# Conditioning by rows in three float32r passes, input checks moved behind, output chunks ended one by one

## The chip, the cores and the metric

The kernel runs on one core of a Trainium2 chip. The metric is the device time of one execution in microseconds (us), as the median of several runs. A profiled execution gives, beside its own time, the start and end of every instruction on the engines: PE (TensorE; PEld is its weight load), DVE (VectorE), ACT (ScalarE), POOL (GpSimd), and SP, which here only issues DMAs.

## The reference

The input x has 8 rows of 128 tokens with 512 features, all float32. Two layers are added to it, each a conditioning followed by a feed-forward network. Cut to the core:

```python
# layer 0
base = einsum('btd,od->bto', x, W)
logits = einsum('btd,ed->bte', x, Wr) + 5.0 * one_hot(language_ids)      # 8 experts
gates = softmax over the two largest logits, zero for the others
lora = einsum('bter,bte,eor->bto', einsum('btd,erd->bter', x, A), gates, B)
c = base + 2.0 * lora
w = scales[g_idx] * (nibbles - (zeros[g_idx] + 1))                       # 4-bit weights
x = x + down(silu(gate(c)) * up(c))                                      # 512 -> 1376 -> 512
# layer 1
c = einsum('bsi,boi->bso', x, weight[adapter_ids])                       # one of 8 matrices by row
c = rms_norm(c) * ln_w
x = x + down(silu(gate(c)) * up(c))                                      # 512 -> 1792 -> 512
```

## The kernel before

All activations are kept transposed: features on the 128 partitions in four chunks (KC = 4), the 1024 tokens along the free axis, in two halves of 512 (NTB = 2, TB = 512). A half has four rows of x.

A product that must be exact to float32 can be had in two ways here. A plain float32 matmul is one instruction that the hardware runs as two records. Or both operands are split into a high part in float32r, a low part and a scaled combination (`a3[0]`, `a3[1]`, and a third), and float32r matmuls over the parts are summed in PSUM, with a rescale of the PSUM bank between the passes. The layer 1 network works with three such passes (L924, L988). The layer 0 network needs two, because its dequantised integers are exact, and rescales the sums from one group of scales to the next by `ratio` and `ratio_d`.

The condition of layer 0, one half after the other: `experts(tb)` (L286) multiplies each row by `wa`, the router and all low-rank A matrices side by side (136 columns). `gated(tb, banks)` computes on DVE the two best experts and their softmax, with one Exp on ACT (L315), and multiplies the low-rank products by the gates (`hg`). `condition(tb, hg)` computes `base` in plain float32 (L349), transposes `hg` on PE (L346), copies it to SBUF and adds the low-rank part with `bT` (L359). `split_condition` writes the high part on ACT (L619) and the low part on DVE (L620); these feed the gate and up products of layer 0 (L485). x arrives by chunk and half (`load_x`, L214), chunks 1 and 3 on ACT's queue, the others on SP's; it lies in `xT`, which is also the residual. `wT` is loaded in two halves on the two queues. Until x is there, 13 idle matmuls of 512 columns keep PE busy (L236).

While `base` runs, DVE unpacks zeros and dequantises the first four chunks of gate and up weights (`queue_zeros`, `queue_weights`). After the second half's `experts`, DVE works out the row numbers for gathers (`indices`), the `ratios`, and a `verdict`: whether the group indices and scales are such that the fast way applies. `judge` sums the verdict over the partitions with a tiny matmul (L660) and writes a flag (L661). Then POOL starts the first gathers of layer 1's adapter matrices (`first_w1`, L268).

The orders of PE, DVE and ACT are written out by hand (`manual_schedule`). In the networks, a small planner decides when queued DVE and ACT work is issued: `spent` moves a clock by 0.2326 us for each matmul, `pump` issues queued tasks whose time has come, and `flush` issues a named task at the latest where it is needed. POOL and the DMA queues follow the scheduler's order.

In layer 0, `down` (L532) runs for each output chunk m over halves (`tb`), and inside over the high and the low part of h. `last_chunk_and_down` interleaves the last gate and up chunk with the first products of the last down block. Layer 1 begins with `adapt` (L870) and `normed` (transposes, L889) for each row, then gate and up in 14 chunks, with `down` (L988) after each of four blocks. In the last block, the third pass runs by halves: all four output chunks for the first 512 tokens, then all four for the second; each of the eight results is added to `xT` (L1000) and stored by a DMA of 256 KB (L1021), even m on ACT's queue and odd m on SP's.

At the very end every engine loads the flag (`values_load`, L1061) and branches (L1062): a second, general network in plain float32 follows in the program and runs only if the flag is set. With these inputs it doesn't run.

Of the kernel before, what the change touches and what calls it, by code (L numbers as in the profile page):

```python
# [27 lines left out]
NWARM = 13  # L28
# [38 lines left out]
GU_PLACE, FLAG_PLACE = 64, 24  # L67

AFTER = 0.3

# [13 lines left out]
def network(tc: tile.TileContext, a, out, by_groups, flag=None):  # L84


    with ExitStack() as ctx:
        network_in(ctx, tc, a, out, by_groups, flag)


def network_in(ctx, tc, a, out, by_groups, flag):
# [111 lines left out]

    xsrc = a["xT"].rearrange("(c p) t -> p c t", p=P)
    wa = cp.tile([P, KC, E + E * R], F32, name="wa")
    wT = cp.tile([P, KC, D], F32, name="wT")
    bT = cp.tile([P, D], F32, name="bT")
    g_idx = const.tile([P, KC + NJ0], I32, name="g_idx")
# [3 lines left out]
    def load_x(c, tb):  # L212
        cols = slice(tb * TB, (tb + 1) * TB)
        (nc.sync, nc.scalar)[c % 2].dma_start(out=xT[:, c, cols], in_=xsrc[:, c, cols])  # L214

    nc.sync.dma_start(out=wa, in_=a["WA"])
    for c in (1, 0, 3, 2):
        load_x(c, 0)
    for half, eng in enumerate((nc.sync, nc.scalar)):
        cs = slice(2 * half, 2 * half + 2)  # L220
        eng.dma_start(out=wT[:, cs, :], in_=a["WT"][:, cs, :])
    nc.sync.dma_start(out=ids[:, 0, :], in_=a["ids0"].partition_broadcast(P))
    for c in (1, 0, 3, 2):
        load_x(c, 1)
    nc.scalar.dma_start(out=bT, in_=a["BT"])
# [4 lines left out]


    ones = cp.tile([P, TB], BF16, name="ones")
    nc.vector.memset(ones, 1.0)
    idle = bank("idle")
    for _ in range(NWARM):
        nc.tensor.matmul(idle, lhsT=ones[:, :P], rhs=ones, start=True, stop=True)  # L236
# [41 lines left out]
    def experts(tb):  # L278

        got = []  # L280
        for i, ps in enumerate(banks_of("experts", TB // T // 2)):
            ps = ps[:, : 2 * (E + E * R)].rearrange("p (b n) -> p b n", b=2)
            for k in range(2):
                b = tb * (TB // T) + 2 * i + k
                for c in range(KC):
                    nc.tensor.matmul(  # L286
                        ps[:, k, :],
                        lhsT=xT[:, c, b * T : (b + 1) * T],
                        rhs=wa[:, c, :],
                        start=(c == 0),  # L290
                        stop=(c == KC - 1),
                    )
            got.append(ps)
        return got
# [42 lines left out]
    def condition(tb, hg, meanwhile=None):  # L337


        small = pair("hgT")  # L340
        hgT = cp.tile([P, TB], F32, tag="hgT", bufs=2, name="hgT_sb")
        base = banks_of("base", KC)
        for m in range(KC):
            if m == KC - 1:
                for i in range(TB // T):
                    nc.tensor.transpose(small[:, 0, i * T : (i + 1) * T], hg[:, i, :], ident)  # L346
                nc.scalar.copy(hgT, small[:, 0, :])
            for c in range(KC):
                nc.tensor.matmul(  # L349
                    base[m],  # L350
                    lhsT=wT[:, c, m * P : (m + 1) * P],
                    rhs=xT[:, c, tb * TB : (tb + 1) * TB],
                    start=(c == 0),
                    stop=False,
                )
        if meanwhile is not None:
            meanwhile(small[:, 1, :])
        for m in range(KC):
            nc.tensor.matmul(  # L359
                base[m], lhsT=bT[:, m * P : (m + 1) * P], rhs=hgT, start=False, stop=True  # L360
            )
        return base
# [31 lines left out]
    def by_groups_of_scales():  # L394
# [26 lines left out]
        )  # L421

# [51 lines left out]
        def ratios():  # L474
            for r, s in ((ratio, sc), (ratio_d, scd)):

                nc.vector.tensor_tensor(r, s[:, :, 1:], s[:, :, 1:], ALU.mult)
                nc.vector.tensor_scalar(r, r, LEAST**2, None, ALU.is_lt)
                nc.vector.tensor_tensor(r, r, s[:, :, 1:], ALU.add)
                nc.vector.reciprocal(r, r)  # L480
                nc.vector.tensor_tensor(r, r, s[:, :, :-1], ALU.mult)
# [47 lines left out]
        def down_product(ps, m, k, tb, first):  # L529
            n = CH0[k]  # L530
            for i in range(2):
                nc.tensor.matmul(  # L532
                    ps[:, tb],
                    lhsT=wds[k][:n, m * P : (m + 1) * P],
                    rhs=h2[k][i][:, tb],
                    start=(first and i == 0),
                    stop=(i == 1),
                    skip_group_check=not first,
                )
            spent(2)  # L540
# [5 lines left out]
        def down(k0, k1):  # L546

            sums = [pair("down") for _ in range(KC)]
            for k in range(k0, k1):
                flush(f"h{k}")  # L550
                for m in range(KC):
                    if m == 1:
                        flush(f"h{min(k + 2, k1 - 1)}")
                    for tb in range(NTB):
                        down_product(sums[m], m, k, tb, k == k0)
                    if k == k1 - 1:
                        down_final(xT[:, m, :].rearrange("p (b t) -> p b t", b=2), m, sums[m], k)
                    else:
                        rescale(sums[m], ratio_d[:, m, k : k + 1])

        def last_chunk_and_down():
# [16 lines left out]
            def first(m):  # L578
                for tb in range(NTB):
                    down_product(sums[m], m, j - 2, tb, True)  # L580
                rescale(sums[m], ratio_d[:, m, j - 2 : j - 1])

            def second(m, tbs=range(NTB)):
                for tb in tbs:
                    down_product(sums[m], m, j - 1, tb, False)
# [24 lines left out]
            for tb in range(NTB):  # L610
                for m in range(KC):
                    down_product(sums[m], m, j, tb, False)
                    down_final(xT[:, m, tb * TB : (tb + 1) * TB], m, sums[m][:, tb], group)

        def split_condition(tb, base):
            cols = slice(tb * TB, (tb + 1) * TB)
            for m in range(KC):
                hi, lo = (x[:, m, cols] for x in a3)
                nc.scalar.activation(hi, base[m], AF.Copy, scale=HSCALE)  # L619
                nc.vector.tensor_tensor(lo, base[m], hi.bitcast(F32), ALU.subtract)  # L620
# [25 lines left out]
        with tc.manual_schedule(engines={EngineType.PE, EngineType.DVE, EngineType.Activation}):  # L646
            hg = gated(0, experts(0))
            queue_zeros(0, 4, "zeros")
            for j in range(4):
                queue_weights(j, f"w{j}")  # L650
            flush("w3")
            split_condition(0, condition(0, hg))
            hg = gated(1, experts(1))
            indices()
            ratios()
            count = verdict()

            def judge(ps):
                met = ps[:1, :1]
                nc.tensor.matmul(met, lhsT=count[:, 0:1], rhs=count[:, 1:2], start=True, stop=True)  # L660
                nc.vector.tensor_scalar(flag[:1], met, float(NGOOD * P), None, ALU.is_lt)  # L661

            split_condition(1, condition(1, hg, judge))
            cond_stack.close()
            first_w1()
# [36 lines left out]
            queue_down(*BLOCKS0[2], "d8")  # L702
            down(*BLOCKS0[1])
            ready(PAIRS0[4])
            gate_up_pair(8, 9)
            ready(PAIRS0[5])
            last_chunk_and_down()


    def in_float32():  # L710
        gp_stack = ExitStack()
        gp = gp_stack.enter_context(tc.tile_pool(name="gp", bufs=1, side="left"))
        ax = gp.tile([P, KC, NT], F32, name="ax")
        for tb in range(NTB):
            hg = gated(tb, experts(tb))
            base = condition(tb, hg)
            for m in range(KC):
                nc.scalar.copy(ax[:, m, tb * TB : (tb + 1) * TB], base[m])
        indices()
        cond_stack.close()  # L720
        h0 = h_stack.enter_context(tc.tile_pool(name="h0", bufs=1, side="right")).tile([P, NJ0, NT], F32, name="h0")
# [66 lines left out]
        nc.sync.dma_start(out=ln_w, in_=a["ln_w"])  # L788
        first_w1()
# [4 lines left out]
    last_silu = [None]  # L794

# [42 lines left out]
    def first_w1():  # L838
        pools["w1"] = w1_stack.enter_context(tc.tile_pool(name="w1", bufs=1, side="right"))
# [46 lines left out]
    def normed(b, nx):  # L886
        pt = bank("nxT")
        for c in range(KC):
            nc.tensor.transpose(pt[:, c * T : (c + 1) * T], nx[:, c * P : (c + 1) * P], ident)  # L889
        raw = ad.tile([P, KC, T], F32, tag="raw", bufs=2, name="raw")  # L890
# [90 lines left out]
    def down(j0, j1):  # L981

        sums = [pair("down") for _ in range(KC)]
        last = j1 == NJ1

        def one(m, tb, j, which):
            for i in which:
                nc.tensor.matmul(  # L988
                    sums[m][:, tb],
# [7 lines left out]

        def done(m, x, ps):
            charge("dve", took("dve", ps.free_size()))
            nc.vector.scalar_tensor_tensor(x, ps, -EPS, x, ALU.mult, ALU.add)  # L1000


        for js in (range(j0, j1 - 1), range(j1 - 1, j1)):
            for m in range(KC):
                for tb in range(NTB):
                    for j in js:
                        one(m, tb, j, (0, 1))
                if j1 - 1 in js:
                    rescale(sums[m], HLSCALE)
        halves = [slice(0, 1), slice(1, 2)] if last else [slice(0, 2)]  # L1010
        for tbs in halves:
            for m in range(KC):
                for tb in range(tbs.start, tbs.stop):
# [179 lines left out]
```

## Time and profile before

| what | us |
|---|---|
| median of 3 runs | 444.04 (443.54 to 444.15) |
| profiled execution, its own time | 444.17 |
| its span, first to last instruction | 442.3 |
| start of the first experts product after the DMA wait | 8.06 |
| start of the first layer 0 gate product on the chain | 50.81 |
| start of layer 1's first gate product on the chain | 205.33 |
| end of the last PE work | 434.77 |
| PE, DVE, ACT, POOL busy | 431.1, 292.9, 213.1, 9.0 |

The profile is of one execution. A line of the table of groups gives the source line, the engine, the operation, what it writes from what it reads, shapes, the count, busy time and the mean time of one, then how long the engine was idle just before these instructions and what ended that idle time. The chain that ended last is followed back from the last instruction, each time to what released it. A float32 matmul appears as two records. A q behind an engine's name means its sequencer or its DMA queue.

### The profile page before, as it was taken

How to read it: one execution, taken by the hardware profiler on the slowest of the kernel's cores; microseconds unless marked ns; L12 is line 12 of the kernel's file. 1: busy time of each engine (PE TensorE's matmuls, PEld its weight loads, DVE VectorE, ACT ScalarE, POOL GpSimd, SP SyncE). 2: the span in 40 equal slices, each digit the busy share in tenths (PEclk: the TensorE clock that was granted, in tenths of full speed). 3: DMA queues.
4: the chain of work that ended last, by engine and by line, in shares of the span. 5: the costliest groups of instructions: out<-in, count | busy, mean ns of one | idle time of the engine just before them, and what ended most of it. 6: DMA issues, size and time to landing. Idle time of an engine off the chain costs nothing.

```text
span 442.3 us, 4678 instructions
## 1 busy us (share of the span) xinstructions
PE 431.1 (97%) x1799; PEld 326.5 (74%) x1799; DVE 292.9 (66%) x418; ACT 213.1 (48%) x242; POOL 9.0 (2%) x20
## 2 busy tenths in 40 slices
PE   7999999999999999999999999999999999999993
PEld 4464578888888866456888888888888888888882
DVE  0767379997999668877449926379626477634643
ACT  1020388867886766446487322475131471325320
POOL 0000200000000000210000000000000000000000
PEclk9999999999999999999999999999999999999998
DMA  8830170101000002870403301113001110000005
GB/s 284 295 96 1 39 294 0 48 20 36 1 0 0 1 0 96 288 282 1 144 0 106 133 0 41 47 50 95 30 1 47 48 50 24 0 1 0 1 0 196
DMA packets 12269, 30.96 MB, mean 70 GB/s; under 512 B 2640, under 2 KB 5200, under 8 KB 11216
## 3 DMA queue, kind: packets, MB, share of 16 engines
q1 hardware_dynamic: 9648, 19.32, 13.5%
q0 software_dynamic: 1152, 8.39, 5.1%
q10 hardware_dynamic: 1440, 2.88, 1.7%
q8 instruction: 16, 0.26, 0.2%
q14 instruction: 13, 0.11, 0.1%
HBM read 28.49 MB, written 2.10 MB: 69 GB/s over the span
## 4 chain that ended last, share of the span: by engine, by line
PE 91%; DVE 4%; DMA 1%; ACT 1%; issue 0%; SPq 0%; DVEq 0%; ACTq 0%
PE gate L924 17%; PE up L924 17%; PE down L988 16%; PE gate L485 9%; PE down L532 8%; PE up L485 8%; PE base L349 6%; PE adapt L870 5%; PE experts L286 2%; PE base L359 2%; DMA xT<-in_xT 1%; DVE xT L1000 1%; DVE xT L544 1%; PE nxT L889 1%; ACT sl L501 1%; DVE h L504 1%
## 5 line engine op out<-in xcount | busy, mean ns | idle before, releaser
L924 PE MATMUL gate<-a,w 128*128 128x512 f32 x336 | 81.7, 390 | 0.0
L924 PE MATMUL up<-a,w 128*128 128x512 f32 x336 | 81.4, 389 | 0.0
L988 PE MATMUL down<-h,d 128*128 128x512 f32 x336 | 76.8, 389 | 0.0
L924 PEld LDWEIGHTS up<-a,w 128*128 128x128 f32 x336 | 63.1, 188 | 13.1
L988 PEld LDWEIGHTS down<-h,d 128*128 128x128 f32 x336 | 63.1, 188 | 13.1
L924 PEld LDWEIGHTS gate<-a,w 128*128 128x128 f32 x336 | 62.7, 188 | 13.5 <-ACT gate L174 0.6
L941 DVE SCALAR_TENSOR_TENSOR h<-up,sl 128x1024 f32<-128x1024 f32 (+1 forms) x16 | 17.5, 1091 | 50.9 <-PE up L924 44.5
L485 PE MATMUL gate<-a,dq 128*128 128x512 f32 (+1 forms) x176 | 48.0, 394 | 0.2
L485 PE MATMUL up<-a,dq 128*128 128x512 f32 (+1 forms) x176 | 47.3, 391 | 0.0
L532 PE MATMUL down<-h,wd 128*128 128x512 f32 (+1 forms) x176 | 42.3, 394 | 0.8 <-DVE h L188 0.7
L532 PEld LDWEIGHTS down<-h,wd 128*128 128x128 f32 (+1 forms) x176 | 32.5, 188 | 9.7 <-DVE h L188 1.1
L485 PEld LDWEIGHTS gate<-a,dq 128*128 128x128 f32 (+1 forms) x176 | 32.4, 185 | 9.0 <-DVE a L620 0.8
L485 PEld LDWEIGHTS up<-a,dq 128*128 128x128 f32 (+1 forms) x176 | 32.5, 185 | 7.7 <-ACT sl L501 0.2
L198 ACT ACTIVATE h<-h 128x1024 fp32r<-128x1024 f32 (+1 forms) x25 | 26.4, 1054 | 15.9 <-DVE h L941 15.5
L188 DVE TENSOR_TENSOR h<-h,h 128x1024 fp32r<-128x1024 f32 (+1 forms) x25 | 30.4, 1217 | 3.4 <-ACT h L198 3.4
L938 ACT ACTIVATE sl<-gate 128x1024 f32<-128x1024 f32 (+1 forms) x16 | 14.7, 918 | 35.7 <-PE gate L924 35.7
L174 ACT ACTIVATE gate<-gate,ratio 128x1024 f32<-128x1024 f32 (+1 forms) x24 | 26.0, 1085 | 11.6 <-PE gate L485 11.6
L870 PE MATMUL adapt<-w,xT 128*128 128x512 f32 x64 | 28.7, 594 | 0.0
L174 ACT ACTIVATE gate<-gate 128x1024 f32<-128x1024 f32 (+1 forms) x15 | 13.8, 923 | 30.8 <-PE gate L924 30.8
L349 PE MATMUL base<-xT,wT 128*128 128x512 f32 x64 | 28.1, 592 | 0.0
L176 DVE TENSOR_SCALAR down<-down 128x1024 f32<-128x1024 f32 x8 | 9.9, 1232 | 26.2 <-PE down L988 26.2
L174 ACT ACTIVATE up<-up,ratio 128x1024 f32<-128x1024 f32 (+1 forms) x21 | 22.7, 1082 | 5.5 <-PE up L485 5.5
(121 smaller groups left out, 442.6 us busy)
## 6 DMA issues: line engine op xcount, KB each, us to landing
wgu<-in_wgu SPq DMA_DIRECT2D x14, 512.0 KB, 3.4
wd<-in_wd SPq DMA_DIRECT2D x6, 512.0 KB, 3.7
qw<-in_qw_gu SPq DMA_DIRECT2D x5, 512.0 KB, 4.2
xT<-in_xT ACTq DMA_DIRECT2D x4, 256.0 KB, 6.0
xT<-in_xT SPq DMA_DIRECT2D x4, 256.0 KB, 5.6
qwd<-in_qw_d SPq DMA_DIRECT2D x2, 512.0 KB, 5.4
out<-xT ACTq DMA_DIRECT2D x4, 256.0 KB, 3.8
out<-xT SPq DMA_DIRECT2D x4, 256.0 KB, 3.9
```

The lines of the kernel that those rows point to most:

```text
L174: nc.scalar.activation(ps, ps, AF.Copy, scale=by)
L176: nc.vector.tensor_scalar(ps, ps, by, None, ALU.mult)
L188: nc.vector.tensor_tensor(lo, x, hi.bitcast(F32), ALU.subtract)
L198: nc.scalar.activation(hi, x, AF.Copy, scale=HSCALE)
L349: nc.tensor.matmul(base[m], lhsT=wT[:, c, m * P : (m + 1) * P], rhs=xT[:, c, tb * TB : (tb + 1) * TB], start=(c == 0), stop=False,)
L485: nc.tensor.matmul(ps, lhsT=dqs[j][:, c, half, :], rhs=a3[i][:, c, tb * TB : (tb + 1) * TB], start=(c == 0 and i == 0), stop=(i == 1), ski ...
L532: nc.tensor.matmul(ps[:, tb], lhsT=wds[k][:n, m * P : (m + 1) * P], rhs=h2[k][i][:, tb], start=(first and i == 0), stop=(i == 1), skip_gro ...
L870: nc.tensor.matmul(ps, lhsT=xT[:, c, b * T : (b + 1) * T], rhs=wt[:, c * D : (c + 1) * D], start=(c == 0), stop=(c == KC - 1),)
L924: nc.tensor.matmul(ps, lhsT=w3[j][i][:, c, half * P : (half + 1) * P], rhs=a3[i][:, c, tb * TB : (tb + 1) * TB], start=(i == 2 and c == 0) ...
L938: nc.scalar.activation(sl, ps, AF.Silu, scale=1.0 + EPS)
L941: nc.vector.scalar_tensor_tensor(h, ps, 1.0 + EPS, sl, ALU.mult, ALU.mult)
L988: nc.tensor.matmul(sums[m][:, tb], lhsT=d3[j][i][:, m * P : (m + 1) * P], rhs=h3[j][i][:, tb], start=(i == 0 and j == j0), stop=(j == j1 - ...
```

## The change

x is loaded a second way: `xb`, the eight rows one by one (256 KB each, alternately on ACT's and SP's queue), laid out by the host. `xT`, now the residual alone, is loaded later by `load_residual` in two DMAs of 1 MB behind `qzd` on SP. `wT` comes by output chunk in four DMAs and `bT` behind them, all on SP. The 26 idle matmuls have 128 columns.

`experts` of both halves come first. `base` is computed in three float32r passes: x and W are split into high, low and combined parts. Shares of the work: `x_high`, `x_scaled`, `w_high`, the scaling of `bT` and the rescale of the sums on ACT; `x_low` of half 0, `w_low` and `w_diff` on DVE; `x_low` of half 1 and `x_diff` of both on POOL. `kept` saves the second half's experts to SBUF so that its PSUM pair is free. The passes of the two halves alternate. `split_condition` treats two output chunks at a time. `ratios` is called in two parts.

`indices` and `first_w1` move to the second down block of layer 0, `verdict` into its last chunk, `judge` into the first `normed` of layer 1. Layer 0's `down` runs over the parts outside and the halves inside. The flag is loaded ahead of layer 1's last down, with a branch hint for PE, DVE and ACT, and the branch at the end falls through into the second network. The last down ends one output chunk after another, only the last one by halves; the first half of a chunk is stored from ACT's queue, the second from SP's. The second network is changed to match.

The instruction streams of the two kernels show what isn't in the diff: POOL runs `x_diff(0)` before `x_low(1)`, then `x_diff(1)`; the first product of base's second pass of half 1 waits for ACT (`x_scaled(1)`), the first of the third pass of half 0 for DVE, ACT and POOL; one rescale of an up sum moves from DVE to ACT beside `indices`; the ten DVE instructions of `verdict` stand right ahead of the last chunk's h.

```diff
-NWARM = 13
+NWARM = 26
...
+FETCHED = [EngineType.PE, EngineType.DVE, EngineType.Activation]
...
-    for c in (1, 0, 3, 2):
-        load_x(c, 0)
...
+    for b in range(B):
+        (nc.scalar, nc.sync)[b % 2].dma_start(
+            out=xb[:, b].rearrange("p c t -> p (c t)"), in_=a["xb"][b]
+        )
+        if b == 3:
+            nc.sync.dma_start(out=ids[:, 0, :], in_=a["ids0"].partition_broadcast(P))
+    for m in range(KC):
+        nc.sync.dma_start(out=wT[:, m, :], in_=a["WT"][:, m, :])
+    nc.sync.dma_start(out=bT, in_=a["BT"])
...
+    def x_high(tb):
+        for b in rows(tb):
+            nc.scalar.activation(x_parts(tb, b)[0], xb[:, b], AF.Copy, scale=HSCALE)
+
+    def x_low(tb, eng):
+        for b in rows(tb):
+            hi, lo, _ = x_parts(tb, b)
+            eng.tensor_tensor(lo, xb[:, b], hi.bitcast(F32), ALU.subtract)
+
+    def x_scaled(tb):
+        for b in rows(tb):
+            lo = x_parts(tb, b)[1]
+            nc.scalar.activation(lo, lo.bitcast(F32), AF.Copy, scale=1.0 / EPS)
+
+    def x_diff(tb):
+        for b in rows(tb):
+            hi, lo, di = x_parts(tb, b)
+            nc.gpsimd.tensor_tensor(di, hi.bitcast(F32), lo.bitcast(F32), ALU.subtract)
...
+    def base_products(base, tb, m, i):
+
+        for c in range(KC):
+            nc.tensor.matmul(
+                base[m],
+                lhsT=wT3[i][:, m, c * P : (c + 1) * P],
+                rhs=x_parts(tb)[i][:, c, :],
...
+            nc.scalar.activation(root, eps, AF.Exp)
+            exp0 = experts(0)
+            x_high(0)
+            x_low(0, nc.vector)
+            x_scaled(0)
+            exp1 = experts(1)
+            for m in range(2):
+                w_high(m)
+            hg0 = gated(0, rows_of(exp0))
+            for m in range(2, KC):
+                w_high(m)
+            kept = cp.tile([P, 2, 2 * (E + E * R)], F32, name="kept")
+            nc.scalar.copy(kept, exp1[:, :, : 2 * (E + E * R)])
+            x_high(1)
+            x_low(1, nc.gpsimd)
+            x_diff(0)
+            scale_bT()
+            pairs0, base0 = base_sums()
+            for m in range(KC):
+                base_products(base0, 0, m, 0)
+            hgT0 = turned(hg0, exp0[:, 0, :])
+            for m in range(KC):
+                w_low(m)
+                base_products(base0, 0, m, 1)
+            hg1 = gated(1, [kept[:, i].rearrange("p (b n) -> p b n", b=2) for i in range(2)])
+            x_scaled(1)
+            x_diff(1)
+            for ps in pairs0:
+                rescale_base(ps)
+            pairs1, base1 = base_sums()
+            for i in range(2):
+                for m in range(KC):
+                    base_products(base1, 1, m, i)
+            for ps in pairs1:
+                rescale_base(ps)
+            for m in range(KC):
+                w_diff(m)
+                base_products(base0, 0, m, 2)
             queue_zeros(0, 4, "zeros")
             for j in range(4):
                 queue_weights(j, f"w{j}")
+            flush("w2")
+            ratios(ratio, sc)
+            for i in range(2):
+                for m in range(2 * i, 2 * i + 2):
+                    low_rank(base0, hgT0, m)
+                split_condition(0, pairs0[i], i)
+            ratios(ratio_d, scd)
             flush("w3")
...
+            base_products(base1, 1, 0, 2)
+            hgT1 = turned(hg1, base0[0])
+            for m in range(1, 3):
+                base_products(base1, 1, m, 2)
+            for i in range(2):
+                for m in range(2 * i, 2 * i + 2):
+                    if m == KC - 2:
+                        base_products(base1, 1, KC - 1, 2)
+                    low_rank(base1, hgT1, m)
+                split_condition(1, pairs1[i], i)
...
             for i in range(2):
+                for tb in tbs:
...
+            queue("dve", "indices", 1.7, indices)
             down(*BLOCKS0[1])
+            flush("indices")
+            first_w1()
...
+            queue("dve", "verdict", 1.3, lambda: count.append(verdict()))
             last_chunk_and_down()
+            flush("verdict")
...
+        if last:
+            for fn in (first, ended):
+                for m in range(KC - 1):
+                    fn(m)
+            for m in range(KC - 2):
+                added(m)
+                for tb in tbs:
+                    store(m, tb)
+            m = KC - 1
+            banks[m, 1] = pair("down")[:, 1]
+            for tb in tbs:
+                passes(m, (tb,), every, (0, 1))
+                rescale(banks[m, tb], HLSCALE)
+            added(m - 1)
+            for tb in tbs:
+                store(m - 1, tb)
+            for tb in tbs:
+                passes(m, (tb,), every, (2,))
+                done(m, xT[:, m, tb * TB : (tb + 1) * TB], banks[m, tb])
+                store(m, tb)
+            return
...
+            if j1 == NJ1 and by_groups:
+                again.append(nc.values_load(flag[:1, :], min_val=0, max_val=1))
+                tc.mark_branch_hint_location("again", hint=again[0], engines=FETCHED)
             down(j0, j1)
...
-    with tc.If(again > 0, preferred_fallthrough_block=False, name="again"):
+    with tc.If(again[0] > 0, preferred_fallthrough_block=True, label="again", name="again"):
```

## The prediction

> **What bounds the kernel now.** I read the page first (shares of busy time), then the chain of waits in order of time, then windows by stage, then the tail's queue instructions. The page:
>
> ```profile
> span 442.3 us, 4678 instructions
> ...
> PE 431.1 (97%) x1799; PEld 326.5 (74%) x1799; DVE 292.9 (66%) x418; ACT 213.1 (48%) x242; POOL 9.0 (2%) x20
> ...
> PE 91%; DVE 4%; DMA 1%; ACT 1%; issue 0%; SPq 0%; DVEq 0%; ACTq 0%
> ```
>
> TensorE is nearly the whole path, so only three things pay: less PE work, an earlier first matmul, a shorter tail. The chain in order of time (start, length, what) shows the head of the kernel:
>
> ```profile
> 1.67 6.36 DMA xT<-in_xT
> 8.06 3.51 PE experts L286 x28
> 11.58 10.30 PE base L349 x24
> 21.88 0.44 PE hgT L346 x4
> 22.31 3.44 PE base L349 x8
> 25.75 3.43 PE base L359 x8
> 29.18 3.71 PE experts L286 x32
> ...
> 47.06 0.12 PE hgT L660 x2
> 47.18 3.63 PE base L359 x8
> 50.81 1.05 PE gate L485 x4
> ...
> 231.68 3.63 PE gate L924 x16
> ```
>
> Read: a DMA holds the first product to 8.06; from there PE never rests until the first gate product at 50.81. A float32 matmul of 512 columns is two records, 3.44/8 = 0.430 each, so 0.86 us; a float32r one is 3.63/16 = 0.2267 us. The windows by stage give 22 us of DVE and 4.5 us of ACT work in the head, POOL none. The tail (PE ends at 434.77) is shown by the stores' landing times and by the final branch:
>
> ```profile
> DMA to landing us min/median/max: 2.1/3.9/4.7
> ...
> L1062 SPq EVENT_SEMAPHORE  x8: 17/17/17, 436.9 to 440.4; - x8
> ...
> L1062 PEldq COMPARE_BRANCH  x2: 95/2282/4468, 434.2 to 435.0; - x2
> ```
>
> The last store is issued at 435.5 and SP waits for landings until 440.2; PE's branch over the second network takes 4.47 us, to 439.5, and DVE drains at 440.1. Two limits end together; 2 us of barrier follow.
>
> [...]
>
> **Part 1, earlier start.** The windows moved 234 GB/s at 2 to 4 us, 397 at 4 to 6, 389 at 6 to 8, 355 at 8 to 10: 0.50, 1.29, 2.07, 2.78 MB in all. wa and eight rows are 2.38 MB, moved by 8.9; chunks landed up to 1.3 us after their bytes were due (the one at 8.03), so the last row lands at 10.2 to 10.7. wa and row 0 land at about 4.7 (wa took 3.9 from 0.74). A row's experts are eight records at 3.31/28 = 0.118, 0.95 us; eight rows from 5.3 end at 12.9 (12.0 to 14). Before, half 0 alone ended at 11.58. The 26 small idle matmuls end near then too: 0.107 us of streaming each, 0.15 of weight load, 3 to 4.5 us from 1.3.
>
> **Part 2, base in float32r.** 32 float32 matmuls (27.5 us) become 96 at 0.2267 (21.8): 5.7 off PE. From 12.9, in the order that the instruction streams show: base0 pass 0, 3.63, to 16.5; four transposes 0.44; pass 1 to 20.6; base1 passes 0 and 1, 7.25, to 27.9; base0 pass 2 to 31.5; its low rank, four at 0.86, to 34.9; base1 pass 2, transposes and low rank, 3.63 + 0.44 + 3.43, to 42.4. With 0.8 for cross-engine latencies the gate product starts at 43.2 instead of 50.81: 7.6 gained.
>
> The cover. ACT issues four DMAs instead of six, and adds 21 copies of 512 columns at 0.63 (L898), 4 rescales at 1.05, the kept copy 0.65, beside 4 wide splits at 1.08: some 25 us in 42. Its Exp for gated(0) now stands behind w_high(1), thus behind wT chunk 1 (lands about 12.2), so hg0 comes at 15.6, wanted at 16.5. DVE: x_low 4, w_low 4, w_diff 4 at 0.684 (L899), 8.2; two gated of 4.7; zeros 1.7; four dequantised chunks of 0.47 + 2 x 0.67, 7.3; ratios 2.7; three split lows at 1.22, 3.7: 33 us from 5.4, so 38.4 without a wait; with those for Exp and the low rank the third ends at 42.1. **DVE is 0.3 us from being the bound**, with about 2 us of waits that can absorb delay. POOL runs x_diff(0), then x_low(1), then x_diff(1), twelve at 1.2: x_low(1) can't start before x_high(1) (15.6) and ends about 20.5; x_scaled(1) on ACT at 23.2; PE wants it at 24.2. Behind PE's wait for it stands all of base0 pass 2.
>
> **POOL against DVE** is the unknown. Lower bound 0. Upper: strict alternation, each of the twelve blocking one two-input DVE operation (gated has ten, w_low and w_diff eight). Following that through the order, w_low ends at 24.0, hg1 at 33.6, w_diff at 36.4, the first split at 46, the gate product at 52.8 + 0.8: 10.4 later. [...] I take 1.5, since most DVE work of the stage falls in the reach of its own waits; both ends go into the range.
>
> **Part 3, the rest.**
> - First gate and up pieces ran 4.1 us for 3.63 waiting for the splits (L620); the first split now ends ahead: 0.5 gained (0 to 0.5).
> - Down with tb inside: the low part is wanted two matmuls later; at 155.09 PE waited for it (DVE h L188), 0.45 gained (0 to 0.7), no instruction added.
> - indices (1.8 us) goes behind the wd differences at 144, ahead of a 0.9 idle; one rescale moves to ACT. verdict (1.4) goes where DVE idles 2.63 before h L504. Both zero; 1.3 lost if the cover is missed. First gathers leave POOL at about 137, need some 11 us for 3 MB (203 GB/s and up in such stages), wanted at 166: zero.
> - The judge moves to the first normed: its 0.6 (46.47 to 47.11) was inside 50.81 and returns: -0.6 (0 to -0.8).
> - The residual x, 2.1 MB, goes behind qzd on SP; eight row issues, four wT and bT on SP push shifts, ids and qw by a few issues of 0.33 to 0.45. qz and qw now are wanted at 26, not 18: zero, and its x is wanted only in the first down.
> - Flag loads stand ahead of the last down (PE 1.04, DVE 1.20, ACT 0.89). PE's ran 1.8 us ahead of its array at the old place; queued behind are the products. I take -0.3 (0 to -1.3).
> - Tail: done(2) of 1.22 and two of 0.63 end 1.25 after PE instead of 0.72, but only one 256 KB store is then in flight: landing 2.1 to 2.7 instead of 4.7[...]. -0.5 + 2.0 to 2.6, less what queues ahead: +1.6 (0 to 3).
>
> Sum: 7.6 - 1.5 + 0.5 + 0.45 - 0.6 - 0.3 + 1.6 = 7.75. The profiled execution took 444.17 (span plus 1.87), 0.13 over the median of 444.04: 444.17 - 7.75 - 0.13 = 436.3.
>
> **Rivals.**
> 1. Mild interference, as summed: 436.3. Its own range is 433 (no interference, the tail's 3 us) to 440. For it: PE's head is one unbroken chain. Chance 0.58.
> 2. Half the alternation, 5 us instead of 1.5: 439.8. For: DVE is nearly full there. Chance 0.18.
> 3. [...] DVE becomes the bound of the head, gated(1) and w_diff being its place; 10.4 - 1.5 = 8.9 more than the sum: 445.2, slower. It decides once the interference takes over 1.5 + 7.75 = 9.25 us, some 0.8 for each of the twelve. [...] Chance 0.14.
> 4. No tail gain, flag loads in full: 436.3 + 1.6 + 1.0 = 438.9. Chance 0.06.
> 5. Rows don't arrive faster than halves did, experts end at 15: the first part doesn't do what it says, and 2.1 are lost: 438.4. Chance 0.04.
>
> About 0.2% (0.9 us) is what a measurement of this kernel can tell from no change. Faster: cases 1, 2, 4, 5 and a sliver of 3, 0.87; same 0.05; slower 0.08. The range 433 to 443 reaches over cases 1, 2, 4 and 5 with the spread of 2, and leaves out 3 and what lies under 433.
>
> **What would show it.** First gate product at 43 to 45; base records 96 at 0.2267; experts to about 12.9; POOL operations near 1.2 without DVE gaps named after them; last landing within 5 us of PE's end. Wrong if PE idles in base1 pass 1 or base0 pass 2 with DVE or POOL as releaser, or the span's gain sits elsewhere.

## The result, and the profile after

The changed kernel takes **445.5 us** (442.96 to 446.3 in 22 runs), the one before 444.04 (443.54 to 445.17, 22 runs): a ratio of 1.0028, 95% interval 1.0019 to 1.0037. It is slower by some 1.3 us, where 436.3 was forecast. The profiled execution took 445.95, with a span of 444.1.

The page of the changed kernel (span, busy time and instructions of each engine, then each engine's share of the chain that ended last):

```profile
span 444.1 us, 4836 instructions
...
PE 428.7 (97%) x1844; PEld 336.6 (76%) x1844; DVE 306.9 (69%) x421; ACT 231.1 (52%) x268; POOL 25.4 (6%) x32
...
PE 85%; DVE 10%; ACT 1%; DMA 1%; issue 1%; DVEq 0%; ACTq 0%
```

PE has 2.4 us less to do than before, but its share of the chain fell from 91% to 85%, and DVE's rose from 4% to 10%. POOL has gone from 9.0 to 25.4 us. The chain in order of time (start, length, what) shows where DVE took over:

```profile
0.75 4.04 DMA xb<-in_xb
...
4.83 5.63 PE experts L290 x32
...
15.74 6.60 DVE wT L377 x4
...
29.03 1.23 DVE second L331
...
41.89 1.23 DVE a L673
43.16 1.12 PE base L407 x4
44.27 3.41 PE base L387 x8
47.69 2.52 PE base L413 x4
...
52.84 0.92 PE gate L541 x4
```

The first product starts at 4.83 instead of 8.06, as the change intends. But from about 10 to 43 the chain runs through DVE, and the first gate product of layer 0 comes at 52.84, 2.0 later than before (50.81). Layer 1's first gate product follows at 207.18 (before 205.33) and PE ends at 436.69 (before 434.77): the loss is made in the first 53 us and carried to the end.

Two things are visible in that stretch. First, four `w_low` operations (L377) take 6.60 us, and `second`, of 32 elements, 1.23 us. The table of groups of DVE and POOL for 5 to 33 us (busy, mean ns | idle before) says the same:

```profile
L377 DVE TENSOR_TENSOR wT<-wT,wT 128x512 fp32r<-128x512 f32 x4 | 6.7, 1729 | 0.0
L380 DVE SCALAR_TENSOR_TENSOR wT<-wT,wT 128x512 fp32r<-128x512 f32 x4 | 2.5, 686 | 0.0
```

```profile
L371 POOL TENSOR_TENSOR xd<-a,a 128x512 fp32r<-128x512 f32 x8 | 10.0, 1285 | 10.0 <-ACT a L366 10.0
L361 POOL TENSOR_TENSOR a<-xb,a 128x512 fp32r<-128x512 f32 x4 | 6.4, 1629 | 2.0 <-ACT a L356 2.0
```

L377 and L380 have the same shape; the first runs beside POOL's work and takes 1729 ns, the second runs after it and takes 686. Second, PE's clock. The windows of PE (length, busy time, matmuls, granted clock, DMA share, GB/s):

```profile
40.00:43.00 3.00, 0.27 (x2) 0.89 0.28 100
43.00:46.00 3.00, 2.84 (x9) 0.50 0.00 0
46.00:49.00 3.00, 3.00 (x6) 0.50 0.53 151
```

PE waits 2.9 us, and then works at half its clock for six (the clock as the profile gives it, 1.00 being full): in the chain, eight float32r products take 3.41 us (0.43 each; 0.23 at a clock of 1.00).

The tail, by the landing times of SP's and ACT's stores and by SP's waits and PE's branch at the end:

```profile
DMA to landing us min/median/max: 2.5/3.0/3.9
...
L1227 SPq EVENT_SEMAPHORE  x8: 17/17/17, 441.8 to 442.4; - x8
...
L1227 PEldq COMPARE_BRANCH  x1: 407/407/407, 434.6 to 434.6; - x1
```

PE's branch fell from 4.47 us to 0.41. From PE's end to the span's end it is still 444.1 - 436.69 = 7.4 us, against 7.5 before.

### The profile page after: what moved, and what is told of

It is laid out like the page before. It is cut to its first block, busy times and chain, and to the rows that moved or that the text cites. A ratio compares the mean times of both kernels' runs of the same rounds, so it can differ in the third digit from the quotient of the medians.

```text
span 444.1 us, 4836 instructions
## 1 busy us (share of the span) xinstructions
PE 428.7 (97%) x1844; PEld 336.6 (76%) x1844; DVE 306.9 (69%) x421; ACT 231.1 (52%) x268; POOL 25.4 (6%) x32
## 4 chain that ended last, share of the span: by engine, by line
PE 85%; DVE 10%; ACT 1%; DMA 1%; issue 1%; DVEq 0%; ACTq 0%
PE gate L1055 17%; PE up L1055 17%; PE down L1120 17%; PE gate L541 9%; PE down L589 8%; PE up L541 8%; PE adapt L998 5%; DVE wT L377 1%; PE experts L290 1%; PE base L387 1%; PE base L413 1%; DMA xb<-in_xb 1%; DVE dq L442 1%; PE nxT L1018 1%; DVE xT L601 1%; ACT sl L557 1%
## 5 line engine op out<-in xcount | busy, mean ns | idle before, releaser
L175 ACT ACTIVATE down<-down 128x1024 f32<-128x1024 f32 (+1 forms) x10 | 9.2, 923 | 35.8 <-PE down L1120 35.8
L175 ACT ACTIVATE up<-up,ratio 128x1024 f32<-128x1024 f32 (+1 forms) x22 | 23.9, 1085 | 4.9 <-PE up L541 4.9
L1137 DVE SCALAR_TENSOR_TENSOR xT<-down,xT 128x1024 f32<-128x1024 f32 (+1 forms) x17 | 19.6, 1161 | 9.3 <-PE down L1120 9.1
```

The lines of the kernel that those rows point to most:

```text
L175: nc.scalar.activation(ps, ps, AF.Copy, scale=by)
```

## The experiments

The theory (A): POOL's operations hold up DVE's, DVE then sets the head, and PE pays. Rivals: (B) PE waits for POOL's results themselves, because POOL is slow; (C) DVE's own 33 us of work are too much for the head, POOL or not.

### POOL's work left out, and POOL's work done for nobody

`r1_no_pool` takes out POOL's twelve operations; the third pass reads the high part instead of the combined one, so its result is not x's third part, while PE does the same number of products (its edit is the one shown). `r2_pool_unread` is the same, but POOL does all twelve and nobody reads them.

```diff
-            x_low(1, nc.gpsimd)
-            x_diff(0)
...
-            x_scaled(1)
-            x_diff(1)
+            x_scaled(1, True)
...
-                rhs=x_parts(tb)[i][:, c, :],
+                rhs=x_parts(tb)[0 if by_groups and i == 2 else i][:, c, :],
```

> The twelve POOL operations of the condition are left out: x_low(1) and x_diff aren't computed, the third pass reads the high part of x, x_scaled(1) reads the high part; PE, ACT and DVE do as many instructions as in the changed kernel. Theory A[...]: first layer 0 gate product at 42.5 to 45 instead of 52.8, time 435 to 438. Theory B, PE waits for POOL's results because POOL is slow: the same. Theory C, DVE's own work fills the stage and POOL does no harm: gate at 51 to 53, time 444 to 446.

> As r1_no_pool, but POOL does its twelve operations at their old places and writes the results where nobody reads them, so no engine waits for a POOL result before the last split. Theory A: DVE is blocked as before, gate product at 50 to 53, time 443 to 446. Theory B: nobody waits, so like r1, 435 to 438. Theory C: 444 to 446, as r1.

Measured: r1 438.4 us (ratio to before 0.9889, 0.9864 to 0.9914), r2 446.28 (1.0034, 1.0012 to 1.0056), both 0.3 to 0.4 us above what theory A allowed. The chain of r1:

```profile
13.23 3.72 PE base L390 x16
...
17.39 14.87 PE base L390 x64
...
40.74 1.03 ACT a L675
...
44.73 0.93 PE gate L544 x4
```

and of r2:

```profile
52.51 0.93 PE gate L544 x4
```

In r1, PE is the chain from 8.33 to 40.74 without a break, and the gate product starts at 44.73. A wait of 1.2 us for L675 comes from the edit: the high part that the third pass reads is overwritten by the next split. r2 has the same edit and the same wait of 1.2 us, so it drops out of the difference. So POOL's twelve operations cost 52.51 - 44.73 = 7.8 us at the gate product and 7.9 us in the medians, though nobody waits for what they write. `w_low` (L380 here) takes 684 ns in r1 and 1313 in r2. B falls. C falls as well: DVE's other work is the same in r1, and PE doesn't wait for it. **A is shown**, as far as it says that POOL's operations hold up DVE's and that PE pays. Why they do, these two runs don't show.

### Which POOL operations hold up which DVE operations

`p1_probe` is the kernel before with dummy POOL operations of 128x512 in its head.

```diff
+            dummy = cp.tile([P, 4, TB], F32, name="dummy")
+            for k in range(6):
+                nc.gpsimd.tensor_tensor(dummy[:, 0, :], xT[:, 2, :TB], xT[:, 3, :TB], ALU.subtract)
+            for k in range(10):
+                nc.gpsimd.tensor_copy(dummy[:, 1, :], xT[:, 2, :TB])
+            for k in range(12):
+                nc.gpsimd.memset(dummy[:, 2, :], 0.0)
```

> The kernel before, with dummy GpSimd operations of 128x512 beside its head: six two-input subtractions, ten copies, twelve memsets; nobody reads their result. It asks which of them stretch which DVE operations. Theory A: a two-input DVE operation standing beside a GpSimd subtraction takes the rest of that operation (about 1.2 us) more; a memset, which reads nothing, stretches none; copies lie between. Reads of PSUM by DVE are not stretched by any. DVE has slack in the kernel before, so the time stays within 2 us of 444.

It took 443.8 (one run), as expected. Groups of DVE from 10 to 26 us in the probe:

```profile
L366 DVE TENSOR_SCALAR zq<-qz 128x512 uint16<-128x512 uint16 x8 | 4.5, 632 | 0.0
L319 DVE TENSOR_TENSOR w<-w,ex 128x4 f32<-128x4 f32 x1 | 1.2, 1181 | 0.0
...
L316 DVE TENSOR_SCALAR dif<-ex 128x4 f32<-128x4 f32 x1 | 1.0, 956 | 0.3 <-ACT ex L315 0.3
```

In the kernel before, the same three take 287, 161 and 171 ns. A two-input subtraction on POOL takes 1.26 us (the prediction's 1.2 stood on no run; in the changed kernel `x_diff` takes 1.285 and `x_low(1)` 1.629); L319, standing beside one, 1.18 for 0.16. L316 and L319 end with the subtraction beside them: at 16.03 and 17.80 us, for 16.00 and 17.77 on POOL. Reads of PSUM (L305, beside a copy) keep their 0.17, Max (L309, beside a subtraction) its 0.155. The expectation missed in one point: L366 (one uint16 input) goes from 287 to 632 ns while POOL does copies and memsets in turn. Among memsets alone, L386 with two SBUF inputs keeps its 0.69, and the uint16 shift L369 takes 0.83 and 0.66 for 0.48. So a memset, which reads nothing, did hold up some DVE operations.

What sets the DVE operations that are held up apart from the others is not shown: the profile gives their lengths and times alone.

### POOL's work given to DVE

`r3_dve` lets DVE do all twelve. Their place in DVE's order is new as well: `x_low(1)` and `x_diff(0)` stand behind `w_low`.

```diff
-            nc.gpsimd.tensor_tensor(di, hi.bitcast(F32), lo.bitcast(F32), ALU.subtract)
+            (nc.vector if by_groups else nc.gpsimd).tensor_tensor(di, hi.bitcast(F32), lo.bitcast(F32), ALU.subtract)
```

> The changed kernel with GpSimd's twelve operations given to DVE as they are: 12 x 0.68 = 8.2 us more on DVE, GpSimd idle. Theory A with its price: [...] gate product at about 50 to 51.5, time 442.5 to 444, below the changed kernel's. Rival[...]: gate product at 53 or later, time 446 or more.

Measured: 442.18 us (0.9948, 0.9934 to 0.9963), gate product at 49.52, both a little better than expected. By theory A, POOL's operations cost DVE some 10 us in the changed kernel (10.2, summed up below), more than the 8.2 of doing their work; by the rival, less. With 8.2 us more for DVE to do, the kernel is 3.3 us faster than with the work shared between two engines (the order, which also changed, is not priced apart). DVE still sets the head, though: PE waits 2.9 us for its first split and runs at a mean clock of 0.60 from 43 to 46.

### PE's order around the wait

Half the clock after a wait could be the wait's consequence, or chance. `f1_fill` leaves DVE and POOL as they are and only moves PE work from behind the wait to ahead of it.

```diff
-            base_products(base1, 1, 0, 2)
-            hgT1 = turned(hg1, base0[0])
-            for m in range(1, 3):
+            for m in range(KC):
                 base_products(base1, 1, m, 2)
+            hgT1 = turned(hg1, base0[0])
...
-                    if m == KC - 2:
-                        base_products(base1, 1, KC - 1, 2)
                     low_rank(base1, hgT1, m)
```

> The changed kernel with GpSimd's work left as it is; only PE's order differs: all four third-pass products of half 1 stand ahead of the transposes that wait 2.9 us for DVE's first split, instead of one. DVE and GpSimd do the same work in the same order, so the split still comes at about 43.2. If PE's cost is that wait and the half clock after it (PE clock 0.50 from 43 to 49 in the changed kernel): the wait shrinks to 0.2 to 0.8, the clock stays at 1.00, PE has 2.8 us less to do after 43.2, gate product at 47.5 to 49, time 440.5 to 442.5. Rival, that the half clock comes without the wait: clock again about 0.5 from 43 on, gate product at 50 or later, 443.5 and more. Rival, that DVE's later work bounds the gate whatever PE does: gate still at 52 to 53, 445.

Measured: 442.46 us (0.9957, 0.9944 to 0.9971), the gate product at 48.60. The windows of PE in f1 (columns as above):

```profile
43.00:46.00 3.00, 2.15 (x9) 1.00 0.00 0
46.00:49.00 3.00, 3.00 (x10) 1.00 0.41 101
```

The first split ends at 43.5, as late as in the changed kernel. The wait is down to 0.2 us (and 0.7 for the copy of hgT), the clock stays at 1.00, and 3.0 us come back. In this pair the half clock goes with the wait, then, but not each time: with the same head and the same 2.9 us wait, the profiles of `t2_tail_turns` and `w1_warm` below show 1.00 throughout and a gate product at 49.40 and 49.33. The low clock also varies in length. Windows of 0.2 us give its start and end: 42.36 to 49.19 in the changed kernel and 45.52 to 52.34 in `r6_three` (6.8 us each), 42.41 to 45.82 in r2, 41.99 to 45.40 in r3 and 43.51 to 46.92 in `t1_tail_halves` (3.4 us each), so once or twice the same 3.4 us. It need not start within the wait: in r3 PE had been at work again for 0.9 us. Of the changed kernel's 22 runs, 20 have a mean clock of 0.989 to 0.993 over the whole kernel, f1's five 0.996 to 0.997. That fits one or two such spans in most runs (1.7 or 3.4 us lost in 444 are 0.004 or 0.008), but a mean doesn't say where the clock was low.

The length of the wait alone doesn't settle it: 2.8 us (r2) to 3.1 us (r6) came with half the clock in five profiles, 2.9 us without it in two. Behind shorter waits (1.8 us for L380 in r3, 1.2 in r1, 0.2 and 0.7 in f1, 0.6 in `r7_order` below) the clock stayed at 1.00. What sets the low clock off, and its length, is not shown.

### Rows first with base in plain float32

`r4_rows_fp32` keeps the rows, both halves' experts first and all that follows the head, with base as 32 plain float32 products and nothing on POOL.

```diff
+    def base_float32(base, tb, m):
+        for c in range(KC):
+            nc.tensor.matmul(
+                base[m],
+                lhsT=wT[:, m, c * P : (c + 1) * P],
+                rhs=xb[:, tb * (TB // T) : (tb + 1) * (TB // T), c, :],
```

> x by rows and both halves' experts first, but base in plain float32 as in the kernel before, no split of x and W, no POOL work in the stage; all else as changed. PE alone then sets the head: experts to 13 to 14, 27.5 of base, 6.9 of low rank, 0.9 of transposes: gate at 48.5 to 49.5 and time 441 to 442.5 under theories A and B, since DVE has slack. Under theory C the same, as DVE has 17 us less to do. A gate product after 51 would say that rows first is itself the loss.

Measured: 441.47 us (0.9938, 0.9924 to 0.9953). Its chain is PE alone:

```profile
44.74 3.43 PE base L423 x8
48.17 1.16 PE gate L551 x4
```

What the change does without float32r brings the gate product from 50.81 to 48.17, 2.6 us, and 2.6 us in the medians, about as expected.

### The tail

`t1_tail_halves` ends the last two chunks by halves, chunk 2 first; `t2_tail_turns` takes them in turns, half by half.

```diff
-            added(m - 1)
...
+            for tb in tbs:
+                for k in (m - 1, m):
+                    passes(k, (tb,), every, (2,))
+                    done(k, xT[:, k, tb * TB : (tb + 1) * TB], banks[k, tb])
+                    store(k, tb)
```

(t2; in t1 the two loops change places.)

> The changed kernel with the last two output chunks, not only the last, ended and stored by halves. If the tail is set by the bytes that remain once PE has ended (1.05 MB in the last four stores, at some 384 GB/s), two of these stores leave about 0.7 us earlier: 0.4 to 0.9 us less than the changed kernel, last landing within 5.0 of PE's end. [...]

> The changed kernel with its last two output chunks computed in turns by half (chunk 2 half 0, chunk 3 half 0, chunk 2 half 1, chunk 3 half 1), so that PE writes one pair of PSUM banks while DVE reads another, and the stores are spread. If the bytes still to move at PE's end set the tail: last landing about 1 to 1.4 us earlier against PE's end, time 444.1 to 444.6. If the final branch and the drain behind it set it: no change, 445.3 to 445.7.

t1: 445.68 us (1.0024, 1.001 to 1.0038), no gain; PE waited 0.85 us for DVE (L1137), as its next products write the pair of PSUM banks that DVE was reading, so t1 says nothing on the bytes. t2: 444.45 (1.0011, 1.0 to 1.0022), inside what was expected. In its profile PE ends at 434.51 and the span at 440.9: 6.4 us for 7.4. So with the stores spread, what follows PE's end is 1.0 us shorter, as expected if the bytes left to move set it. A gain for the whole kernel isn't shown. From the gate product to the span's end t2 takes 391.5 us (440.9 - 49.40); with the changed kernel's tail it is 391.3 (444.1 - 52.84), in w1_warm 391.2 (440.5 - 49.33) and in f1_fill 392.3 (440.9 - 48.60). And the medians, 444.45 against 445.5, differ by less than a low clock in the head, present or not, makes.

### Longer idle work ahead

`w1_warm` changes `NWARM = 26` to `34` in the changed kernel.

> The changed kernel with 34 idle products ahead instead of 26 (0.114 us each, so until about 4.9 instead of 4.02). If the slow first experts (64 records in 9.32 us, 0.146 each, where 0.118 was forecast) come from the gap between the last idle product and the first row: experts take 7.6 to 8.2 us and end at 12.4 to 13.0. If they come from rows that land late: no change. The kernel's time does not tell it, since DVE bounds its head: 444 to 446.

The experts' 64 records took 8.79 us (0.137 each; the changed kernel 9.32), although no gap was left ahead of them. Neither side of the expectation held, and 8.79 says little: with 26 idle products the same records took 7.99 us in `r6_three` and 10.04 in `t1_tail_halves`. The gap isn't the cause, or not alone. What sets them apart is seen in PE's weight loads (count, then ns min/median/max, first and last start). The changed kernel's experts, from 6 to 7 us and from 9 to 10, then its low-rank products at the recorded clock of 0.50:

```profile
L290 PEld LDWEIGHTS experts<-wa,xb x6: 332/333/333, 5.7 to 6.8; 128*128 128x128 f32 x6
L290 PEld LDWEIGHTS experts<-wa,xb x10: 190/190/190, 8.9 to 9.9; 128*128 128x128 f32 x10
L413 PEld LDWEIGHTS base<-hgT_sb,bT x4: 194/330/337, 47.1 to 49.2; 128*128 128x128 f32 x4
```

A float32 weight load takes 190 ns at a clock of 1.00 (the seven of L413 from 35 to 38 us too) and some 330 at 0.50. So the first experts' loads, at 332, ran as at half the clock, although the profile gives 1.00 for that stretch. The records become short at about 8.2 us in the changed kernel, 7 in w1_warm, 9.3 in t1_tail_halves and before 5 in r6_three. Why the moment differs stays open. w1_warm took 442.27, a single run, whose head had the full clock after the wait.

### Three passes without the combined parts, then DVE's order

`r6_three` forms the three passes as high by high, high W by low x, low W by high x. No third parts are needed: POOL, `x_scaled`, the rescales and `w_diff` go; DVE does `x_low(1)`.

```diff
-                lhsT=wT3[i][:, m, c * P : (c + 1) * P],
-                rhs=x_parts(tb)[i][:, c, :],
+                lhsT=wT3[(0, 0, 1)[i] if by_groups else i][:, m, c * P : (c + 1) * P],
+                rhs=x_parts(tb)[(0, 1, 0)[i] if by_groups else i][:, c, :],
```

> The changed kernel with its three float32r passes formed differently: high by high, high weights by low x, low weights by high x. Nothing is scaled or combined, so GpSimd's twelve operations, ACT's x_scaled and rescales and DVE's w_diff all go; PE keeps its 96 base records; DVE now forms the low part of half 1 (four operations of 0.68 us). Theory A[...]: DVE's two-input operations run at 0.68, the gate product starts at 43 to 45, time 435.5 to 438. Rival (DVE's own 33 us and its order set the head[...]): gate product at 48 or later, time 441 or more.

Measured: 440.86 us (0.994, 0.992 to 0.9959), gate product at 46.28: between the two. No DVE operation is stretched (L377 686 ns), but in DVE's order two dequantised chunks, a third and both `ratios` stand between the first half's splits and the second's:

```profile
34.34 1.23 DVE L673 TENSOR_TENSOR a<-base,a 128x1024 fp32r<-128x1024 f32 x1 [7.05 <-ACT a L672]
...
45.01 2.35 DVE L673 TENSOR_TENSOR a<-base,a 128x1024 fp32r<-128x1024 f32 x2
```

The number in brackets is DVE's idle time ahead: 7.05 us before the first split. The last two came at 45.01. PE waited 3.1 us for them and then had half its clock from 46 to 52. `r7_order` moves that work into the idle time:

```diff
-            flush("w0")
+            flush("w2")
+            ratios(ratio, sc)
+            flush("w3")
+            ratios(ratio_d, scd)
             for i in range(2):
                 for m in range(2 * i, 2 * i + 2):
                     low_rank(base0, hgT0, m)
                 split_condition(0, pairs0[i], i)
-            flush("w2")
-            ratios(ratio, sc)
-            flush("w3")
-            ratios(ratio_d, scd)
```

> r6_three with one change of DVE's order: the three dequantised chunks and the ratios that stood between the splits of half 0 and half 1 go ahead of half 0's splits, where DVE idled 7.05 us. Nothing is added or removed. If the rest of r6_three's loss is this queue on DVE: PE doesn't wait at the first gate product (3.08 us in r6_three) nor run its next 24 products at 0.43 us for 0.23 (3 us to be had), gate product at 42 to 43, time 434.5 to 437. If the low clock there comes whatever the wait, only the 3 us: 437.5 to 438.5. Rival, that the splits become late because 8 us of work now stand ahead of them: gate at 45 or later, 440 and more.

Measured: **436.66 us** (436.27 to 437.28; 0.9827, 0.9812 to 0.9842). The end of its head's chain:

```profile
35.65 1.14 DVE a L673
...
37.49 2.80 PE base L387 x12
...
43.72 0.69 PE gate L541 x3
```

PE's longest wait after the rows is 0.6 us, and its clock is 1.00 from 40 to 52. The same instructions in another order are 4.2 us faster by the medians. In the two profiles (spans of 439.7 and 434.9) 2.6 of 4.8 us are at the gate product (46.28 to 43.72), most of the rest is the clock behind it. Whether the medians divide in the same way isn't shown: three of r6_three's nine runs have a mean clock of 0.996 or 0.997 and still took 440.8 to 440.9. This version is faster than both kernels.

`r8_best` is r7_order with the tail of t2.

> r7_order with the last two output chunks in turns by half, as in t2_tail_turns, where the time from PE's end to the span's end was 6.4 us for the changed kernel's 7.4. Gains add: 0.8 to 1.1 us under r7_order. If they don't, the same as r7_order within 0.3.

Measured: 436.48 us (436.11 to 439.68; 0.9842, 0.9816 to 0.9868), not to be told from r7_order. In the profiles the tail is 6.4 us for 7.4, but PE ends half a us later (428.0 for 427.5). A gain of 0.8 isn't shown.

## Why the prediction was wrong

**The step that failed is the allowance for POOL against DVE**: "I take 1.5, since most DVE work of the stage falls in the reach of its own waits". It measured 7.8 us (r2 against r1). The bound from above was nearly what came: first split at 46 and gate product at 53.6 by the prediction's strict alternation, 43.1 and 52.84 in the changed kernel. DVE's stretched groups there exceed their times in r6_three by 4 x 1.04 us (L377), and two each by 0.57 (L330), 0.54 (L326), 0.51 and 0.49 (L331), 0.40 (L323) and 0.49 (L309): 10.2 us. Two errors made 1.5 of it:

- The slack was counted once for all. The text itself has DVE "0.3 us from being the bound"; about 2 us of waits could not absorb 10. In the changed kernel the first split ends at 43.1, while PE stands waiting since 40.3.
- Small operations were held to be safe, and only the lengths of large ones weighed. L319 of the probe, 0.16 us by itself, lost 1.0 beside a subtraction, as it ended with it. In the changed kernel POOL does `x_diff(1)`, four operations of 1.27 us on end, from 25.13 to 30.20, and on the chain four operations of `gated(1)` (25.19 to 30.26) take 4.9 us that take 0.7 in r6_three.

**Not in the prediction at all: PE's clock.** In the changed kernel's profile the gate product is 9.6 us behind the forecast (52.84 for 43.2). PE's waits for DVE are 4.8 of them (2.9 for the split, 1.0 and 0.9 for `w_low` and `w_diff`). The products from 43.16 on took 2.8 us more than the same ones do in w1_warm, which had the full clock there (1.12, 3.41 and 2.52 for 0.66, 1.86 and 1.72). The experts ended 1.2 late. Together 8.8; the last 0.8 isn't separated. The clock's share differs between runs: in r2, whose low clock was shorter, the same products lost 1.4 us (1.12, 2.80 and 1.73).

So rival 3, strict alternation with 445.2, named what cost the time (DVE held up by POOL's operations), `gated(1)` as its place, and the right side. Its 8.9 us beyond the sum are not what this alone did: part of the loss is the clock after the wait, the tail's missing 1.5 us came on top, and that the total agrees within 0.3 is partly luck. `w_diff`, its other place, wasn't stretched (L380, 686 ns from 31.19 on); POOL was done at 30.20. Of the signs of being wrong, PE idle in base0 pass 2 with DVE as releaser came, with 0.95 us; the longest wait, 2.9, stood at the transposes of half 1, where no sign was set.

The other terms:

- **Rows and experts first**: right in kind. Rows landed in time in the changed kernel (in r1, r3, r4 and f1 PE waited 0.35 to 0.76 us for one of the later rows). Both halves' experts ended at 14.1 for 12.9, since their records took 0.146 us each on average for 0.118, the first ones about 0.2. In r1 they ended at 13.23. r4_rows_fp32 puts this part, with all that isn't float32r, at 2.6 us.
- **float32r**: right. 64 records in 14.87 us in r1 are 0.232 each, and r7_order, without POOL's operations, has its gate product at 43.72 for the 43.2 forecast, with its passes formed otherwise. The 0.8 for latencies in the forecast stood on no run; in f1 PE's wait for the copy of hgT alone was 0.7.
- **First gate pieces, down, judge**: from the gate product to PE's end the changed kernel takes 383.85 us, the one before 383.96; these three terms and the flag loads sum to +0.05 and gave 0.1. That is luck in part. The first gate and up pieces gained as forecast. PE's wait in the down stage fell only from 0.7 to 0.4 us, and a new one of 0.4 for ACT's `sl` came. The judge's 0.6 was misread: in the prediction's own chain its records take 0.12 (L660).
- **Flag loads**: -0.3 was taken; no wait of PE for them is visible.
- **Tail**: +1.6 was taken (0 to 3), 0.1 came. The branch fell from 4.47 us to 0.41, but four stores, 1.05 MB, were still to move after PE's end, not "one 256 KB store". A landing took up to 3.9 us, not 2.1 to 2.7, and the last store left 1.2 us after PE's end (437.9) where it had left 0.7 after it (435.5). This is rival 4's first half. In t2_tail_turns, with the stores spread, what follows PE's end is 1.0 us shorter (6.4 for 7.4), without a shown gain for the kernel.
- The sum: 6.3 (POOL) and 1.5 (tail) of the 9.2 us missed are these two terms; the rest is the experts' late end and smaller ones that the profiles don't separate. One reading of the prediction was off without entering the sum: DVE's work in the head before is 24.4 us by the windows, not 22.

The chances put 0.14 on the rival that came true and 0.58 on the likeliest. With DVE's slack in the text at 0.3 us, strict alternation deserved the larger share.

## What to carry to other kernels

Work moved from DVE to GpSimd beside a busy DVE cost DVE more here than doing it itself: twelve operations, 8.2 us on DVE, cost it 10.2 on GpSimd. Count the GpSimd operations that meet a DVE operation of the kinds stretched here (two inputs, 16 bits, or L323 with one): with L377 and `gated(1)` a meeting cost DVE about 1.05 us beside an operation of 1.27 to 1.63, for DVE operations of 0.69 us as for those of 0.16 to 0.19. And look at what stands in order behind a wait: the same instructions with PE's products ahead of the wait (f1_fill), or DVE's spare work ahead of the splits (r7_order), gave 3.0 and 4.2 us. A wait of about 3 us often cost twice: in five of the seven profiles that have one (2.8 to 3.1 us), PE also had half its clock for 3.4 or 6.8 us.

## What the hardware showed that was not expected

- The half clock after 2.8 to 3.1 us without work, in five of seven profiles: for 6.8 us in the changed kernel and r6_three, for 3.4 in r2, r3 and t1_tail_halves, not at all in t2_tail_turns and w1_warm.
- DVE operations of four elements and one SBUF input (L316 in the probe, 0.96 us for 0.17), and uint16 ones beside GpSimd memsets (L369, 0.83 for 0.48), are held up too.
- At the start PE works as at half its clock for some us (weight loads of 332 ns for 190) while the profile gives 1.00. Idle products right up to the first row did not bring the experts to their full rate (0.137 us for 0.118).
